# A scan, attention and experts block for four images: the head ordered by hand, mask and residual of the attention as identity matmuls, the group norm at another place in the order

## The chip, the cores and the metric

The kernel runs on one core of a Trainium2 chip. The metric is the device time of one execution in microseconds (us), the median of several executions. PE is the engine of matmuls (PEld its weight loads), DVE the vector engine, ACT the one of activations, POOL GpSimd, SP the one whose queue issues most DMAs. "Tile" here is a named buffer of the program; PSUM is the memory that matmuls write.

## The reference

Four images `x[b]` of 384 channels and 32 x 32 positions (L = 1024 tokens), all in float32. Cut to what matters:

```python
x = x + _L0_conv_ref(_gn(x), ...)          # group norm (32 groups), selective scan, LayerNorm, gelu
t = _to_tokens(x)
t = t + _L1_attn_ref(_ln_t(t), Wq, Wk, Wv)
t = t + _L1_ffn_ref(_ln_t(t), gate_w, gate_b, w1, b1, w2, b2)
```

The selective scan runs over the tokens in four directions k, for 384 channels and 16 states each: `h = h * exp(dt * A) + dt * u * B`, `y = sum over states of h * C`, where dt (softplus of a projection), B and C are projected from the normalised image. The attention has one head of 384, is causal (`where(causal, q k^T * scale, -inf)`, softmax, times v) and is added to t. The last part sends every token through four experts (384 to 1536 to 384, gelu), weighted by a gate of which the two largest of four count.

## The kernel before, in words

A channel group of 32 channels times 4 states fills the 128 partitions. One such group, over all 1024 tokens, is a *unit*; the list `units` has 4 images x 3 blocks of 128 channels (m) x 4 directions (k) x 4 state groups (q) x 4 channel groups (j) = 768. Per unit ACT makes the decay `da` (L442, two units ahead), DVE the product `v` of du = dt*u and B (L449, into PSUM) and the scan `h` (L455), POOL multiplies h by C (L462), and every fourth unit PE sums over states with the matrix `sel` (L487, 16 instructions). The rows of dt and du (128 channels x 1024) and of B and C (`rows`) go out to DRAM and come back spread over the partitions, by DMAs on SP's queue: `dt4` five units ahead, `du4` three, `bc` three (`fetch`, L424 on).

The order of all engines from the first fetches on is written by hand under `tc.manual_schedule()` (L1072): one *tick* t per unit emits the decay of t+2, what was deferred to this tick (`due`), `v` of t, the product of t-1, what stands in `inner`, the scan of t, the sum, the fetches, one step of the preparation of an image, and then other work by generators. A generator yields `("wait", n)` to come back n ticks later or `("pe", n)` to say how many us of PE it has emitted; `go_on` lets the first generator in `waiting` go until the tick's budget is used (`PACE_A` = 4.4 us a tick in attention, `PACE_E` = 3.3 in the experts). Each engine takes its own instructions in the order of emission, and so does SP's queue. PSUM banks (`banks`, 4 of them) and SBUF buffers (`slots`, 8 of them) are taken and given back with the tick; a generator that finds none free waits a tick.

Around the scan:

- **Head** (L140 to L235, `preparation(0)` until its "start", and `fold`). It stands outside the manual schedule, so here the framework orders the instructions. x of image 0 comes on SP's queue, all weights on ACT's. `preparation(b)` (L379): load the image, `groupnorm` (L284: BN_STATS and their sum on DVE, two trips through PE over the groups with `gsel` and `gback`, square root on ACT, normalise on ACT, L312), `project_x` for two pairs of directions (L318: matmuls `pxd`, L328; the two halves of the result copied by ACT to `xd` and `bc`; `bc` stored as `rows`), then `project_dt` (L339) for three blocks and two pairs: matmul, softplus, store, du on DVE (L369), store. In the head this runs up to the first `project_dt`; both pairs' `project_x` come before it. `fold` (L589) then computes g = Wq Wk^T (6 PE groups with ACT copies) and stores it; the first fetches follow.
- **Preparation of image b > 0**: from tick 192 (b-1) + 24 on, one step a tick, group norm included (image b-1 is then being scanned, and image b-2 is in attention).
- **`finish(b)`** (L617): after an image's last unit a LayerNorm (`layernorm`, L517: mean by matmul `mu`, subtract on DVE, L538, squares on ACT, L546, whole width 1024 at once, variance by matmul, L554, reciprocal, spread by matmul `rb`, multiply on DVE, L583), gelu, and the addition of x on DVE (L632).
- **`attention(b)`** (L639), beside the scan of image b+1: LayerNorm, qt and vt (L662, L673), and for eight blocks of 128 queries: `scores` (PE, L691), `softmax` (DVE: add the mask `causal` to the last 128 columns, L702; row maximum, L705; times -scale, L706; ACT: Exp with scale and bias, L710), `normalise` (ACT, L722), `turn` (transposes on PE, copies on ACT, L653), `values` (PE, `po`, L757), and `add` (DVE: three additions of `po` to `yb`, L767, in `inner` of the next tick) with a store.
- **`experts(b)`** (L873): 4 experts x 2 halves of the tokens, `ph` (L947), gelu, `fy` (L972), then DVE (L981, L984).

Work for the last image has no scan beside it: it is a tail.

Of the kernel before, what the change touches and what calls it, by code (L numbers as in the profile page):

```python
# [8 lines left out]
F32 = mybir.dt.float32  # L9
# [38 lines left out]
def hybrid_kernel(  # L48
# [112 lines left out]

    first_x = load_image(0)

    grp = ap0.tile([P, M, C], F32, tag="a0", name="grp")
    nc.scalar.dma_start(grp, group.rearrange("(c p) d -> p c d", p=P))
# [4 lines left out]
    for pair, ks in enumerate(PAIRS):  # L170
        for i, k in enumerate(ks):
            d0, r0 = 64 * pair + 32 * i, 64 - 64 * pair + 32 * i
            for o, w0 in ((d0, 0), (r0, BC0)):
                nc.scalar.dma_start(
                    wx[:, :, pair, o : o + 32],
                    w_x[:, k, w0 : w0 + 32].rearrange("(c p) j -> p c j", p=P),
                )
            nc.scalar.dma_start(wdt[d0 : d0 + R, :], w_dt[:, k, :])
    dtb = const.tile([P, K, M], F32, tag="dtb", name="dtb")
    nc.scalar.dma_start(dtb, dt_bias)  # L180
    lnw = const.tile([P, M], F32, tag="lnw", name="lnw")
    nc.scalar.dma_start(lnw, ln_w)
    lnb = const.tile([P, M], F32, tag="lnb", name="lnb")
    nc.scalar.dma_start(lnb, ln_b)
    dsk = const.tile([P, M, K], F32, tag="dsk", name="dsk")
    nc.scalar.dma_start(dsk, d_skip)
    dsum = const.tile([P, M], F32, tag="dsum", name="dsum")
    nc.vector.tensor_reduce(dsum, dsk, AX.X, ALU.add)
# [3 lines left out]
    nc.vector.tensor_copy(gsel, grp[:, :, :: C // NGRP])  # L192
    gback = const.tile([NGRP, C], F32, tag="gback", name="gback")
    pgb = bank("pgb")
    for m in range(M):
        nc.tensor.transpose(pgb[:NGRP, m * P : (m + 1) * P], gsel[:, m, :], ident)
    nc.scalar.activation(gback, pgb[:NGRP, :C], AF.Copy, scale=float(C // NGRP))


    a_raw = one.tile([P, K * NG, N], F32, tag="yb", name="a_raw")  # L200
    for i in range(NI):
        nc.scalar.dma_start(a_raw[i::NI], a_logs.rearrange("(g d) n -> d g n", d=DJ))
    nc.scalar.activation(a_raw, a_raw, AF.Exp)
    state_i = const.tile([P, NI], F32, tag="state_i", name="state_i")
    nc.vector.tensor_reduce(state_i, ident.rearrange("p (d i) -> p i d", i=NI), AX.X, ALU.add)
    nc.vector.tensor_scalar_mul(state_i, state_i, -1.0)
    a4 = const.tile([P, K * NG, NQ], F32, tag="a4", name="a4")
    nc.vector.memset(a4, 0.0)
    for i in range(NI):
        nc.vector.scalar_tensor_tensor(  # L210
            a4, a_raw.rearrange("p g (q i) -> p g q i", i=NI)[:, :, :, i],
# [947 lines left out]
```

## Time and profile before

The median of 9 runs is 3923.31 us (3918.7 to 3930.33).

| | |
|---|---|
| profiled execution | 3925.99 us |
| its span, first to last instruction | 3924.2 us |
| busy: PE, DVE, ACT, POOL | 3387.2, 3111.6, 1870.3, 1808.1 us |
| mean granted PE clock | 0.890 |
| first L449 of images 0, 1, 2, 3 | 60.4, 800.5, 1633.2, 2463.2 us |
| last L449 | 3250.9 us |
| L455, one scan | 2.285 us |
| L449, one product | 1.233 us |

"Busy" is the sum of an engine's instructions; PE's ends are modelled, so a busy PE isn't PE at its peak. In a table of stretches each engine has its busy us and, in brackets, its instructions. A group of instructions has its line, engine and operation, the tiles out<-in, their shapes and count, then the busy us of all and the mean ns of one, then the idle time of the engine just before them and what ended it. A line of waits has who waited, for whom, us in total, times, and the longest. A line of the timeline has the start, the length and the instruction, with in brackets the idle time before it and what ended it.

### The profile page before, as it was taken

What the parts mean: (1) busy time and instruction counts of PE and PEld (TensorE: products, weight loads), DVE (VectorE), ACT (ScalarE), POOL (GpSimd) and SP (SyncE); (2) the same over time, 40 slices, a digit from 0 to 9 for tenths busy, and PEclk for the clock granted to TensorE, in tenths of its full rate; (3) what the DMA queues carried; (4) which work ended last, traced back from release to release, by engine and by line L of the source; (5) the groups of instructions that cost most, each with busy time, mean ns of one, the idle gap of its engine ahead of it and who ended that gap; (6) DMA issues with size and microseconds to landing.
All of it is one profiled execution on the core that took longest, in us unless ns stands there. A gap on an engine that the chain in (4) does not pass through costs nothing.

```text
span 3924.2 us, 31831 instructions
## 1 busy us (share of the span) xinstructions
PE 3387.2 (86%) x10463; PEld 1369.7 (35%) x10463; DVE 3111.6 (79%) x2348; ACT 1870.3 (48%) x1940; POOL 1808.1 (46%) x776
## 2 busy tenths in 40 slices
PE   5565655558899999988899999788999998999999
PEld 2000100014433334334334334344334344644444
DVE  4999999999899989999999899999999994210000
ACT  5342544444656555545656645545455553332221
POOL 2665666654455556544555556555566651000000
PEclk7555665569999999998899999899999999999999
DMA  5544545453566766544666665535666651132321
GB/s 194 198 146 175 194 155 192 150 183 121 195 213 213 254 206 200 192 158 160 211 223 225 228 226 195 190 105 199 205 207 205 227 189 51 61 90 82 95 82 55
DMA packets 406085, 671.83 MB, mean 171 GB/s; under 512 B 33264, under 2 KB 280352, under 8 KB 405920
## 3 DMA queue, kind: packets, MB, share of 16 engines
q1 hardware_dynamic: 393808, 667.11, 50.0%
q10 hardware_dynamic: 12112, 2.69, 0.4%
q8 instruction: 83, 1.36, 0.1%
q14 instruction: 82, 0.67, 0.0%
HBM read 597.75 MB, written 71.96 MB: 171 GB/s over the span
## 4 chain that ended last, share of the span: by engine, by line
PE 44%; DVE 43%; ACT 5%; issue 5%; DMA 2%; DVEq 0%; POOL 0%; ACTq 0%; SPq 0%; POOLq 0%
DVE h L455 25%; PE ph L947 17%; PE fy L972 15%; DVE v L449 13%; PE y L487 4%; PE pq L662 2%; PE pv L673 2%; PE po L757 1%; ACT da L442 1%; PE ss L691 1%; DMA t2d<-yb 1%; DVE du L369 1%; ACT ht L936 1%; DVE fy L981 1%; ACT L442 1%
## 5 line engine op out<-in xcount | busy, mean ns | idle before, releaser
L462 POOL TENSOR_TENSOR h<-h,bc 128x1024 f32<-128x1024 f32 x768 | 1807.1, 2353 | 1448.5 <-DVE v L449 1345.4
L455 DVE TENSOR_TENSOR_SCAN h<-da,v 128x1024 f32<-128x1024 f32 x768 | 1755.2, 2285 | 84.8 <-DVE v L449 2.4
L442 ACT ACTIVATE da<-dt,a 128x1024 f32<-128x1024 f32 x768 | 877.0, 1147 | 1229.8 <-DVE h L455 1182.5
L972 PE MATMUL fy<-ht,w 128*128 128x512 f32 x2304 | 1027.1, 603 | 1.8 <-ACT dt L361 1.8
L947 PE MATMUL ph<-fx,w 128*128 128x512 f32 x2304 | 1021.4, 599 | 3.6 <-ACT ht L932 3.6
L487 PE MATMUL y<-h,sel 128*32 128x512 f32 x3072 | 710.5, 716 | 331.7 <-POOL h L462 317.9
L449 DVE TENSOR_TENSOR v<-du,bc 128x1024 f32<-128x1024 f32 x768 | 946.7, 1233 | 43.0 <-DMA bc<-rows 14.6
L972 PEld LDWEIGHTS fy<-ht,w 128*128 128x128 f32 x2304 | 439.0, 193 | 582.4 <-issue 563.8
L947 PEld LDWEIGHTS ph<-fx,w 128*128 128x128 f32 x2304 | 433.6, 191 | 577.2 <-issue 527.7
L932 ACT ACTIVATE ht<-ph,b1s 128x512 f32<-128x512 f32 x384 | 257.2, 679 | 496.9 <-PE ph L947 496.5
L487 PEld LDWEIGHTS y<-h,sel 128*32 128x32 f32 x3072 | 117.5, 119 | 875.0 <-POOL h L462 613.9
L981 DVE SCALAR_TENSOR_TENSOR fy<-fy,b2s,tw 128x512 f32<-128x512 f32 x96 | 72.4, 754 | 430.5 <-PE fy L972 430.5
L936 ACT ACTIVATE ht<-ht 128x3072 f32<-128x3072 f32 x64 | 176.8, 2763 | 0.8
L442 ACT ACT_TABLE_LOAD x108 | 138.6, 1283 | 2.0
L691 PE MATMUL ss<-axn,qt 128*128 128x512 f32 (+3 forms) x288 | 108.2, 526 | 15.2 <-ACT pr L710 8.2
L757 PE MATMUL po<-pt,vt 128*128 128x256 f32 x480 | 105.6, 379 | 15.3 <-ACT pt L653 15.3
L757 PEld LDWEIGHTS po<-pt,vt 128*128 128x128 f32 x480 | 90.4, 202 | 31.0 <-ACT pt L653 18.2
L355 PE MATMUL pdt<-xd,wdt 12*128 12x512 f32 x192 | 73.2, 805 | 13.9 <-ACT dt L361 12.2
L691 PEld LDWEIGHTS ss<-axn,qt 128*128 128x128 f32 x288 | 53.3, 204 | 60.7 <-issue 33.8
L984 DVE TENSOR_TENSOR fx<-fx,fy 128x512 f32<-128x512 f32 x96 | 65.9, 686 | 3.3
L936 ACT ACT_TABLE_LOAD x50 | 64.2, 1283 | 0.9
L361 ACT ACTIVATE dt<-pdt,dtb 128x512 f32<-128x512 f32 x96 | 60.6, 683 | 6.2 <-PE pdt L355 5.7
(170 smaller groups left out, 1305.4 us busy)
## 6 DMA issues: line engine op xcount, KB each, us to landing
bc<-rows SPq DMA_DIRECT2D x384, 512.0 KB, 4.8
w<-in_w SPq DMA_DIRECT2D x384, 384.0 KB, 6.0
dt<-dts SPq DMA_DIRECT2D x192, 512.0 KB, 4.2
du<-dts SPq DMA_DIRECT2D x192, 512.0 KB, 6.2
dts<-dt SPq DMA_DIRECT2D x48, 512.0 KB, 3.5
dts<-du SPq DMA_DIRECT2D x48, 512.0 KB, 4.4
fx<-t2d SPq DMA_DIRECT2D x12, 768.0 KB, 6.8
tw<-mkd SPq DMA_DIRECT2D x32, 256.0 KB, 5.9
```

Of the source, the lines that this page charges most:

```text
L442: nc.scalar.activation(u["da"], spread["dt4", n], AF.Exp, scale=a4[:, g, u["q"] : u["q"] + 1])
L449: return nc.vector.tensor_tensor(u["v"], spread["du4", n], spread["bc", n][:, 0, :], ALU.mult)
L455: nc.vector.tensor_tensor_scan(u["h"][:, ::step], u["da"][:, ::step], u["v"][:, ::step], 0.0, op0=ALU.mult, op1=ALU.add,)
L462: product = nc.gpsimd.tensor_tensor(h, h, spread["bc", n][:, 1, :], ALU.mult)
L487: nc.tensor.matmul(y, sel, h, start=first, stop=last, tile_position=(0, jj * DJ))
L691: nc.tensor.matmul(ps[:, : e - o], qt[:, c, i * P : (i + 1) * P], xn[:, c, o:e], start=(c == 0), stop=(c == M - 1),)
L757: nc.tensor.matmul(pv[:, o:], vt[:, j, m * P : (m + 1) * P], pts[step][j // 4][:, j % 4, o:], start=(j == 0), stop=(j == nj - 1),)
L932: nc.scalar.activation(ht[:, f, :], ps, AF.Identity, bias=bias)
L936: nc.scalar.activation(ht, ht, AF.Gelu)
L947: nc.tensor.matmul(ps, tiles[n][:, c, (f % 2) * P : (f % 2 + 1) * P], xns[h][:, c, :], start=(c == 0), stop=(c == M - 1),)
L972: nc.tensor.matmul(pss[m], tiles[n][:, f, :], hts[fh][:, f, :], start=(fh == 0 and f == 0), stop=(fh == 1 and f == FH - 1),)
L981: nc.vector.scalar_tensor_tensor(ps, ps, b2s[:, e, m : m + 1], tw, ALU.add, ALU.mult)
```

## The change

Seven things are changed.

1. **The whole head is under the manual schedule.** x, grp, wx, wdt and dtb come on SP's queue, a_logs alone on ACT's. Exp of a_logs and a dummy Sqrt stand first on ACT. In the group norm of image 0, gsel, its transposes and gback (now a DVE multiply) come after the first block's statistics; block 1 is normalised by DVE. A dummy Softplus and the weights of the scan (`scan_weights`) come before the first projection. Of image 0, DVE makes one of the two copies of pair 0, the read of B and C is issued at once, and `first_dt` makes dt and du for block 0 of pair 0 by halves, storing and fetching direction by direction. Pair 1's projection comes after the start of the ticks.
2. **Weights that are used later, and `fold`, move into the ticks** (`later`, from tick 8 or so), with waits between their steps, on SP's queue. g is scaled by -scale.
3. **The scores come with the sign turned and scaled**: the mask is +1e30, and PE adds it with a matmul of `ident` and `causal` into the last 128 columns. DVE takes a minimum in place of the maximum, and instead of L706 (32 times) a minimum of two columns where a row has two pieces (16 times). Exp has scale -1.
4. **The residual of attention goes in by PE**: a matmul of `ident` and `yb` (256 columns) opens each `po`; ACT copies `po` to `yb` (512 and 256 columns a step), in `due` of the next tick.
5. **Squares of the LayerNorm by halves of 512 columns.**
6. **The preparation of image b steps on as soon as that of b-1 is over**, through load and group norm, and waits only then for tick 192 (b-1) + 24.
7. `fetch` can be told which of its three reads to issue.

The core of the diff:

```diff
+    ctx.enter_context(tc.manual_schedule())
     first_x = load_image(0)
-    nc.scalar.dma_start(grp, group.rearrange("(c p) d -> p c d", p=P))
+    nc.sync.dma_start(grp, group.rearrange("(c p) d -> p c d", p=P))
+    a_raw = one.tile([P, K * NG, N], F32, tag="yb", name="a_raw")
+    for i in range(NI):
+        nc.scalar.dma_start(a_raw[i::NI], a_logs.rearrange("(g d) n -> d g n", d=DJ))
...
+    def group_weights():
+        nc.vector.tensor_copy(gsel, grp[:, :, :: C // NGRP])
+        pgb = bank("pgb")
+        for m in range(M):
+            nc.tensor.transpose(pgb[:NGRP, m * P : (m + 1) * P], gsel[:, m, :], ident)
+        return pgb
...
+    nc.scalar.activation(a_raw, a_raw, AF.Exp)
+    nc.scalar.activation(dump, eps, AF.Sqrt)
...
-        out=causal, in_=causal, compare_op=ALU.is_ge, fill=NEG, base=0,
+        out=causal, in_=causal, compare_op=ALU.is_ge, fill=-NEG, base=0,
...
+    def later():
+        yield "wait", 8
+        for t, src in (
...
+        ):
+            nc.sync.dma_start(t, src)
+            yield "wait", 1
+        yield "wait", 2
+        nc.vector.tensor_reduce(dsum, dsk, AX.X, ALU.add)
+        yield from fold()
@@ groupnorm
+            if b == 0 and m == 0:
+                pgb = group_weights()
             yield "wait", 1
+        if b == 0:
+            nc.vector.tensor_scalar_mul(gback, pgb[:NGRP, :C], float(C // NGRP))
...
+            if b == 0 and m == 1:
+                nc.vector.tensor_scalar(
+                    u[m], u[m], rstd[:, m : m + 1], mean[:, m : m + 1], ALU.mult, ALU.add
+                )
@@ new
+    def first_dt(u, xd):
+        ks = PAIRS[0]
+        dts = [slots.now(f"dt_0_{k}_0", P, L) for k in ks]
+        dus = [slots.now(f"du_0_{k}_0", P, L) for k in ks]
+        pss = {(i, h): banks.now(f"pdt_0_{i}_{h}") for h in range(NH) for i in range(2)}
+        for (i, h), ps in pss.items():
+            r = slice(32 * i, 32 * i + R)
+            nc.tensor.matmul(ps, wdt[r, :P], xd[r, bass.ts(h, 512)], start=True, stop=True)
+        for i, k in enumerate(ks):
+            for h in range(NH):
+                s = bass.ts(h, 512)
+                nc.scalar.activation(
+                    dts[i][:, s], pss[i, h], AF.Softplus, bias=dtb[:, k, 0:1]
+                )
+                nc.vector.tensor_mul(dus[i][:, s], dts[i][:, s], u[0][:, s])
+            nc.sync.dma_start(dts_d[0, k][0, :P, :], dts[i])
+            nc.sync.dma_start(dts_d[0, k][1, :P, :], dus[i])
+            if i == 0:
+                for t in (-5, -4):
+                    fetch(t, ("dt4",))
+                    fetch(t + 2, ("du4",))
+        for t in (-3, -2, -1):
+            fetch(t, ("dt4",))
+            if t < -2:
+                fetch(t + 2, ("du4",))
...
@@ preparation
         yield from groupnorm(b, u)
+        while clock[0] < IMAGE * (b - 1) + 24:
+            yield "wait", 1
         xd = one.tile([P, L], F32, tag="xd", name=f"xd_{b}")
-        for pair in range(2):
-            yield from project_x(b, pair, u, xd)
+        if b == 0:
+            nc.scalar.activation(dump, eps, AF.Softplus)
+            scan_weights()
+        yield from project_x(b, 0, u, xd)
+        if b == 0:
+            fetch(-3, ("bc",))
+            first_dt(u, xd)
+            yield "start", 0
+        yield from project_x(b, 1, u, xd)
@@ layernorm
-            nc.scalar.activation(sq, dst[:, c, :], AF.Square)
             sqs.append(sq)
+        for h in range(n):
+            for c in range(M):
+                s = bass.ts(h, 512)
+                nc.scalar.activation(sqs[c][:, s], dst[:, c, s], AF.Square)
@@ attention
+                if e > i * P:
+                    nc.tensor.matmul(ps[:, e - o - P : e - o], ident, causal, start=False, stop=True)
...
-            last = ss[-1][2]
-            nc.vector.tensor_add(last[:, -P:], last[:, -P:], causal)
...
-                nc.vector.tensor_reduce(nb[:, n : n + 1], ps, AX.X, ALU.max)
-            nc.vector.tensor_scalar(
-                nb[:, 0:1], nb[:, 0:1], nb[:, len(ss) - 1 : len(ss)], -scale, ALU.max, ALU.mult
-            )
+                nc.vector.tensor_reduce(nb[:, n : n + 1], ps, AX.X, ALU.min)
+            if len(ss) == 2:
+                nc.vector.tensor_tensor(nb[:, 0:1], nb[:, 0:1], nb[:, 1:2], ALU.min)
...
+                nc.tensor.matmul(pv, ident, yb[:, m, s], start=True, stop=False)
...
-                for m in range(M):
-                    nc.vector.tensor_add(yb[:, m, s], yb[:, m, s], pos[m])
+                for m in range(0, M, 2):
+                    n = min(2, M - m)
+                    nc.scalar.copy(
+                        yb[:, m : m + n, s],
+                        pos[m // 2][:, : n * TQ].rearrange("p (m t) -> p m t", m=n),
+                    )
...
-            defer(1, add, inner)
+            defer(1, add)
@@ ticks
-            if preps and t >= IMAGE * (B - 1 - len(preps)) + 24:
+        if preps:
```

## The prediction

> **What bounds the kernel now.** First the chain that ended last, then busy time by stretch, cut where the timeline of DVE shows an image's first L449 multiply (60.4, 800.5, 1633.2, 2463.2 us), 72 ticks after the second of these, where image 0's attention is over, and in the tail.
>
> ```profile
> PE 44%; DVE 43%; ACT 5%; issue 5%; DMA 2%; DVEq 0%; POOL 0%; ACTq 0%; SPq 0%; POOLq 0%
> ```
>
> ```profile
> 0.00:60.40 60.40, 33.62 (x103) 17.93 (x103) 11.66 (x33) 26.90 (x35) 1.09 (x8) 0.92 0.63 192
> 60.40:800.50 740.10, 431.99 (x886) 67.55 (x884) 706.70 (x426) 325.55 (x299) 447.71 (x191) 0.60 0.50 178
> 800.50:1145.80 345.30, 276.56 (x1090) 130.66 (x1091) 313.98 (x291) 179.77 (x212) 169.41 (x73) 0.86 0.47 164
> 1145.80:1633.20 487.40, 481.38 (x1445) 192.12 (x1444) 456.71 (x287) 287.40 (x275) 282.82 (x121) 0.99 0.65 221
> 3254.80:3454.50 199.70, 183.21 (x742) 104.36 (x741) 56.76 (x116) 63.44 (x102) 2.38 (x2) 0.95 0.19 61
> 3454.50:3924.20 469.70, 463.76 (x1082) 205.01 (x1080) 36.21 (x59) 99.82 (x102) 0.00 (x0) 1.00 0.27 79
> ```
>
> Columns: stretch, length, then PE, PEld, DVE, ACT, POOL busy, PE clock, DMA share, GB/s. No engine is full in the head. Image 0's scan is DVE-bound: 706.7 of 740.1 us, 95.5%, is DVE full with its gaps. Beside attention DVE falls to 91% and PE to 80% at clock 0.86: they wait for each other. Beside the experts PE is 98.8% and DVE 93.7% busy, both near full. The last experts are PE alone. So the end is set by head + 740 + three intervals of some 830, 830, 788 us + a PE tail of 673.
>
> What ends the head, and what DVE waits for beside image 0's attention:
>
> ```profile
> 59.56 0.33 SPq L613 DMA_DIRECT2D g_d<-g_s  x1
> 60.38 1.23 DVE L449 TENSOR_TENSOR v<-du,bc 128x1024 f32<-128x1024 f32 x1 [14.58 <-DMA bc<-rows]
> 66.37 1.23 DVE L449 TENSOR_TENSOR v<-du,bc 128x1024 f32<-128x1024 f32 x1 [2.36 <-DMA du<-dts]
> ```
>
> ```profile
> DVE ss L702 <- PE ss L691: 6.3, 2, 5.2
> DVE yb L767 <- PE po L757: 5.1, 2, 2.6
> DVE du L369 <- PE ph L947: 3.6, 1, 3.6
> ```
>
> The first multiply waits 14.6 us for rows that stand behind four stores and four reads in SP's queue. The second is late because SP sat at fold's store (L613) until 59.6 before it issued more du reads. The operations that leave DVE:
>
> ```profile
> L767 DVE TENSOR_TENSOR yb<-yb,po 128x256 f32<-128x256 f32 x48 | 17.7, 414 | 26.4 <-PE po L757 26.4
> L702 DVE TENSOR_TENSOR ss<-ss,causal 128x128 f32<-128x128 f32 x32 | 9.4, 293 | 61.9 <-PE ss L691 61.9
> L706 DVE TENSOR_SCALAR nb<-nb 128x1 f32<-128x1 f32 x32 | 6.9, 214 | 1.1
> ```
>
> **What the Trainium skill says.** "TensorE: Matmul & The Clock Gate" (What's actually happening): PE runs at half clock until some 3.4 us of activity. The head agrees: L328's loads came every 0.85 us from 27.1 to 29.7, then every 0.43. "ScalarE: Activation LUTs" (What ACT_TABLE_LOAD costs): 1283 ns a load, and the trace has 1283. "DMA: Bandwidth & Descriptors" (Queues, rings and completion order): SP and ACT each own one ring on the same 16 engines, which take turns between them, so a_logs on ACT's queue still takes time from x on SP's; the trace before never has these two together.
>
> **Head, worked out.** a_logs costs about 4 us of all engines: the DMA share is 80 to 90% from 15.8 to 20.3 us, where little else moves. It now runs beside x (landed by 9.3 us before), and grp comes after x on SP. I take gsel at 11.5 us instead of 5.9. Between zero and full overlap this is 8.5 to 12.5. Then DVE copies gsel (0.24) and has four BN_STATS (0.67) and two aggregates (0.21), 3.1 us; gback by DVE (0.5, as on ACT) and a copy (0.17) bring it to 15.5. The group chain without its waits, from the rows at 11.5 to 20.1: 0.7 to the mean's copy and 1.6 for the way back, 0.8 for four small DVE steps, and 2.3 for the variance: 5.4 us, so 20.9. Sqrt's table is already loaded; 0.3+0.5 us more and the scale stands at 21.7 against 23.9. What is saved (the wait for gback until 15.6, for a_raw's Exp and a table until 22.6) is half spent on the later grp.
>
> From there: three normalise steps of 1.17 on ACT become two, with one on DVE. That tensor_scalar isn't in the trace; "VectorE: DVE Perf Modes" (The perf-mode tier table) lets fp32 tensor_scalar run 2x, so an estimate from 0.61 (half of L449's time) to 1.23 (all of it); 1.0 taken, hidden beside ACT's first. First L328 at 23.0 (25.2 before), half clock for six matmuls, 5.1 us, then 2.6: pair 0 ends at 30.7 (33.0). Only then the order changes: pair 1's projection (6 us of ACT and PE) no longer precedes dt. dt's matmuls of the first half run during the second xd copy; the third of four ends at 33.3 (0.86 each), Softplus (0.65, table loaded by 25.4) at 34.0, the half multiply (0.65) at 34.7: du of k=0 is done there, against 44.7. SP: rows store at 31.5, landing 2.9 later; bc issues for 1.25 to 35.7; two stores to 36.4, landing 3.2 to 4 later (bc's 1 MB goes ahead at about 400 GB/s, as the head's DMA slices reach 390 to 419), 40.4; dt4 and du4 reads issue by 42.2 (1.15 and 0.64) and land some 2.4 us later. First L449 at **44.6**, against 60.4: −15.8. After it 3 MB of stores and reads feed units 1 to 3 at one per 2.6 to 4 us against a 3.7 us tick, so the 2.3 us stall before unit 1 stays about as it was. The fold (18 transposes, 18 matmuls, 9 ACT moves of 0.48, two 576 KB loads, one store) and seven small loads move into the ticks past SP's dt, du and bc reads: ACT is 44% and DMA 50% busy there and da runs two ticks ahead; zero taken. If that cover went, 4.4 us of ACT. **Head −15.8** (−8 to −20).
>
> **Group norm moved.** Per image DVE has 6 x 0.67 + 3 x 0.21 + small steps = 6.0 us. For image 1 nothing moves in kind (tick 24 either way). For image 2 it goes from beside image 0's attention into image 0's scan, where DVE is full: +6.0 there. For image 3 from beside image 1's attention to beside its experts, where DVE has 2% of slack: +4 there. SP is asked for x earlier (three loads of 512 KB, waiting for u's last reader, with dt and bc reads behind): 0, at worst 3 us each.
>
> **Attention beside a scan.** Per image off DVE: 12 x 0.414 + 8 x 0.293 + 8 x 0.214 less 4 x 0.144 = 8.4 us. With L767 goes its wait: 5.1 us for images 0 and 1, 0.4 for image 2. The wait of L702 for PE passes to the reduce behind it (L705) and stays. ACT takes the copies: per image 4 x (0.57 + 0.36) = 3.7 us. ACT's copy now waits for po, and queued behind it are Exp (L710) and pt's copies; da is two ticks ahead, so DVE isn't reached. PE gets 8 identity matmuls of 128 columns and 12 of 256, two instructions each; from 72 of 512 columns in 30.9 us, 0.429 each: 8 x 0.215 + 12 x 0.43 = 6.9 us an image. PE idles 69 us in image 0's stretch (part of it on ACT's pt, 5.5 us, which the identity matmul comes ahead of). Squares by halves: six of 0.62 for three of 1.05, +0.6 us ACT, but the last half ends 1.3 us sooner after DVE's subtract; not counted beside the scan. With the group norm, DVE loses 8.4+5.1+6.0 = 19.5, 19.5 and 8.8 us. What becomes late next is PE (80% busy, +7) and ACT's copy chain, so I keep three quarters: **−14.6, −14.6+4, −6.6**; bounds all (−19.5) and a quarter.
>
> **Tail.** PE gets the same 6.9 us in a PE-bound stretch. Against it: var_at waits 3.7 us for squares, of which 2 goes; po's 2.3 us wait on pt is partly filled by the identity; DVE's two steps of 0.5 ahead of Exp go. **+3** (−1 to +7). Attention's longer budget (12 x 0.43 at 4.4 a tick, 1.2 ticks) pushes some 4 us of image 2's experts past the last scan, into the 5.7 us for which PE waits on L632; zero.
>
> **Sum.** −15.8 + 6.0 − 14.6 − 10.6 − 6.6 + 3 = **−38.6**. The profiled execution took 3925.99 us (span 3924.2 and 1.8 around it), so 3887.4; it stands 2.7 over the median of 3923.31, so **3885** for a median.
>
> **Rivals.** (1) *Attention is paced by the PE-ACT chain, not DVE*: for, PE's waits on ACT (var_at 9.8, pt 5.5) and 80% PE; against, DVE's 91%. Then what DVE loses returns as its waits for PE: head −15.8, group norm +6 +4 −12, half of 4 x 6.9 = +13.8: −4, 3919. 17%. (2) *DVE's waits shrink too*: the waits at L702 (6.3 per image) and du go with a PE that starts values without waiting; −19.5, −15.5, −8.8, three times −4, +6, head −17, tail 0: −66.8, 3857. 17%. (3) *Slower*: image 2's and 3's projections now begin at tick +24, not some 17 later, in the middle of attention; each takes 3 to 4 of 8 slots and 1 or 2 of 4 banks, and attention yields a tick whenever it finds none. Each tick lost beyond the 3 in hand (image 1's experts end at 2501.6, 38 us or 10 ticks into image 3; the next attention waits for L632 until 2522) pushes 3.3 us of experts into the PE tail. It decides from about 12 net ticks (38.6 / 3.3); at 15, 3934. For: they share the pools. Against: preparation held the same pools later in attention. 6%.
>
> **How the numbers follow.** Forecast 60%. The range is 3856 to 3916: it leaves out half of (2), half of (1) and (3). A measurement tells 0.2% (7.8 us) from no change: below 3915.5 lie the forecast, (2) and a third of (1), 0.83; within 0.2% the rest of (1), 0.11; slower, (3), 0.06.
>
> **What would show it.** First L449 near 44.6; image 1's first L449 near 791 (−15.8 + 6); stretches of 72 ticks of about 330 us in place of 345 and 343; no wait at a yb add on DVE; PE from the last scan to the end some 3 us longer. It is wrong if DVE's busy share beside attention falls (then (1)), or if experts reach past tick 13 of an image's scan (then (3)).

## The result, and the profile after

The kernel after the change takes 3910.12 us (median of 9 runs, 3907.11 to 3914.71) against 3922.51 us before (29 runs): a ratio of 0.9969, 95% interval 0.996 to 0.9977. That is 12.4 us gained where 38.6 was forecast: the direction is right and the time lies inside the stated range (3856 to 3916), but two thirds of the gain did not come. The profiled execution has a span of 3909.6 us, 14.6 less than before. All the accounting below is made on spans; where a median says something else, it says so.

The chain that ended last has shifted from PE to DVE:

```profile
DVE 49%; PE 38%; issue 5%; ACT 4%; DMA 2%; DVEq 1%; POOL 1%; SPq 0%; POOLq 0%; ACTq 0%
```

Busy time by stretch, cut at the same events as before (the first product `v`, now L512, of images 0 and 1, 72 ticks later, and so on; columns as in the prediction):

```profile
0.00:49.72 49.72, 20.72 (x59) 10.21 (x59) 14.31 (x37) 13.85 (x17) 1.09 (x8) 0.91 0.64 168
49.72:790.10 740.38, 424.10 (x928) 73.00 (x928) 706.79 (x427) 335.45 (x314) 447.79 (x191) 0.61 0.50 180
790.10:1126.00 335.90, 279.20 (x1125) 136.26 (x1126) 310.25 (x268) 183.66 (x226) 169.64 (x73) 0.88 0.49 174
1126.00:1613.50 487.50, 480.65 (x1454) 192.34 (x1453) 461.30 (x305) 290.73 (x277) 282.81 (x120) 0.98 0.67 226
1613.50:1958.00 344.50, 299.88 (x1210) 147.53 (x1209) 312.27 (x259) 197.22 (x239) 169.75 (x73) 0.94 0.50 172
3237.30:3439.00 201.70, 190.34 (x768) 109.18 (x767) 47.89 (x78) 70.29 (x117) 2.40 (x2) 0.95 0.19 61
3439.00:3909.60 470.60, 464.69 (x1102) 206.90 (x1100) 38.15 (x72) 99.79 (x103) 0.00 (x0) 1.00 0.27 79
```

The head is 10.7 us shorter (60.4 to 49.7) and the attention of image 0 is 9.4 shorter (345.3 to 335.9). The attention of image 1 (1613.5 to 1958.0) is 1.8 us *longer* than before (342.7): PE has more work there (299.9 us, 293.8 before) and DVE less (312.3 us, 317.3 before), yet the stretch didn't shrink. Beside the forecast, part by part:

| part of the span, us | forecast | after | three repairs (below) |
|---|---|---|---|
| head, to the first product | -15.8 | -10.7 | -15.9 |
| scan of image 0 | +6.0 | +0.3 | -1.0 |
| interval of image 1 (image 0's attention and experts) | -14.6 | -9.3 | -14.5 |
| interval of image 2 | -10.6 | +3.0 | +0.1 |
| interval of image 3 | -6.6 | -0.8 | -5.1 |
| tail after the last product | +3 | +2.9 | +3.5 |
| sum | -38.6 | -14.6 | -32.9 |

The last column is the best kernel of the experiments, 3892.03 us: three small edits bring most of what the change seemed to have lost. It lands near the forecast in four rows, but that doesn't make the forecast's steps right: one of the edits changes the order in the head, which the forecast had otherwise.

What DVE waits for in image 0's attention, and then in image 1's (waiting instruction, releaser, us, times, longest):

```profile
DVE nb L780 <- PE ss L771: 6.7, 3, 4.7
DVE nb L780 <- PE ss L766: 2.8, 1, 2.8
```

```profile
DVE nb L780 <- PE ss L771: 11.5, 4, 10.3
DVE axn L601 <- DMA out<-fx: 9.5, 1, 9.5
```

No wait at a yb add is left, as forecast. But the row minimum (L780) waits longer than the mask's add did (6.3 and 6.4 us before): in image 1's attention its longest wait is 10.3 us, where the mask's add waited 5.2. And a wait stands there that was nowhere beside a scan before: the LayerNorm of the attention (L601) waits 9.5 us until the *previous* image's output is stored, since the two share a buffer. The experts of image 0 added their last result at tick 13 of the scan of image 2 before, and now at tick 16.

The long wait for the scores has its reason on PE. DVE stops at 1744.46 us, and what PE does until the scores are there is this (three of its groups), with the end of DVE's wait in this kernel and in the kernel before:

```profile
1744.49 2.74 PE L350 MATMUL pxd<-x,wx 128*128 128x512 f32 x6
1750.95 2.84 PE L350 MATMUL pxd<-x,wx 128*128 128x512 f32 x6
1753.63 0.83 PE L766 MATMUL ss<-axn,qt 128*128 128x128 f32 x6
1754.72 0.29 DVE L780 TENSOR_REDUCE nb<-ss 128x1 f32<-128x128 f32 x1 [10.26 <-PE ss L771]
```

```profile
1759.09 0.30 DVE L702 TENSOR_TENSOR ss<-ss,causal 128x128 f32<-128x128 f32 x1 [5.18 <-PE ss L691]
```

`pxd` is the projection of image 3. With its group norm done early it starts two ticks after the wait for tick +24 ends, at tick +26 of image 2's scan, and stands on PE right ahead of the scores; before, it came at ticks +41 to +47, after them. The 5.58 us of `pxd` cover the 5.1 us by which the wait grew. The experiments below confirm it: with the group norm at its old place this wait is 5.0 to 5.4 us (four kernels), with the early group norm 10.1 to 10.8 (twelve kernels).

Cut into DVE's work and DVE's idle time, the three 72-tick stretches of attention beside a scan give (length = busy + idle, from the traces of the five kernels; "head alone" and "group norm late", the kernel after with the group norm at its old place, are experiments below):

| 72 ticks beside a scan | before | head alone | after | group norm late | three repairs |
|---|---|---|---|---|---|
| attention of image 0 | 345.3 = 314.0 + 31.3 | 340.8 = 314.2 + 26.6 | 335.9 = 310.2 + 25.7 | 340.3 = 311.5 + 28.8 | 334.1 = 307.7 + 26.4 |
| attention of image 1 | 342.7 = 317.3 + 25.4 | 341.6 = 317.4 + 24.2 | 344.4 = 312.2 + 32.2 | 341.6 = 315.1 + 26.5 | 341.2 = 309.4 + 31.8 |
| attention of image 2 | 326.7 = 309.1 + 17.6 | 328.0 = 309.3 + 18.7 | 325.9 = 307.7 + 18.2 | 326.5 = 307.5 + 19.0 | 321.3 = 303.0 + 18.4 |

Three things are read from it. DVE lost only 3.8, 5.1 and 1.4 us of work, not 8.4. The wait at the yb add is gone from the list, but it is no gain in idle time: image 0's idle time is 26.6 us already with the head alone, where the add is still on DVE and still waits 5.1 us. And the 6.8 us of idle time that came in image 1's attention come with the group norm's new place: 25.4, 24.2 and 26.5 with the old one, 32.2 and 31.8 with the new.

**Where DVE's missing saving is.** One row of the new groups is far dearer than it should be, the minimum of two columns that stands in place of the scaling:

```profile
L782 DVE TENSOR_TENSOR nb<-nb 128x1 f32<-128x1 f32 x16 | 13.9, 866 | 0.5
```

I had priced it at 0.144 us. Its sixteen instructions take from 0.158 to 1.712 us each; the four in the tail, where POOL has nothing to do, all take 0.16. The timeline of DVE and then of POOL shows what a long one stands beside:

```profile
2589.33 0.14 DVE L795 RECIPROCAL nb<-nb 128x1 f32<-128x1 f32 x1
2589.45 1.23 DVE L512 TENSOR_TENSOR v<-du,bc 128x1024 f32<-128x1024 f32 x1
2590.59 0.88 DVE L780 TENSOR_REDUCE nb<-ss 128x1 f32<-128x512 f32 x2
2591.51 1.71 DVE L782 TENSOR_TENSOR nb<-nb 128x1 f32<-128x1 f32 x1
2593.15 2.27 DVE L518 TENSOR_TENSOR_SCAN h<-da,v 128x1024 f32<-128x1024 f32 x1
```

```profile
2590.86 2.35 POOL L525 TENSOR_TENSOR h<-h,bc 128x1024 f32<-128x1024 f32 x1 [1.63 <-DVE v L512]
```

The minimum starts at 2591.51, inside POOL's product, and ends at 2593.22; the product ends at 2593.21. "SBUF — State Buffer" (Who interferes with whom) of the Trainium skill says that a DVE instruction with two inputs in SBUF (the memory of all tiles that aren't in PSUM) contends with a POOL instruction that reads SBUF, and that the port pair they share is an exclusive lock. This trace agrees: of the twelve beside a scan, eleven start while a POOL product runs, ten of these take 0.67 to 1.71 us and end within 0.02 us of that product's end, and the eleventh starts in the product's last 0.11 us and takes 0.16. The reduce just before, with its input in PSUM, isn't held up.

### The profile page after: what moved, and what is told of

It is laid out like the page before. It is cut to its first block, busy times and chain, and to the rows that moved or that the text cites. A ratio compares the mean times of both kernels' runs of the same rounds, so it can differ in the third digit from the quotient of the medians.

```text
span 3909.6 us, 32087 instructions
## 1 busy us (share of the span) xinstructions
PE 3385.5 (87%) x10623; PEld 1393.1 (36%) x10623; DVE 3099.6 (79%) x2258; ACT 1887.6 (48%) x1996; POOL 1808.5 (46%) x776
## 4 chain that ended last, share of the span: by engine, by line
DVE 49%; PE 38%; issue 5%; ACT 4%; DMA 2%; DVEq 1%; POOL 1%; SPq 0%; POOLq 0%; ACTq 0%
DVE h L518 29%; DVE v L512 16%; PE ph L1027 14%; PE fy L1052 13%; PE y L550 3%; PE ss L766 2%; PE pq L737 2%; PE pv L748 2%; PE po L832 1%; DVE fy L1061 1%; ACT da L505 1%; PE pxd L350 1%; ACT ht L1016 1%; DVE du L395 1%; DMA du<-dts 1%
## 5 line engine op out<-in xcount | busy, mean ns | idle before, releaser
L1052 PE MATMUL fy<-ht,w 128*128 128x512 f32 x2304 | 1014.6, 597 | 2.7 <-ACT dt L387 0.9
L512 DVE TENSOR_TENSOR v<-du,bc 128x1024 f32<-128x1024 f32 x768 | 947.0, 1233 | 39.4 <-DMA du<-dts 17.4
L550 PE MATMUL y<-h,sel 128*32 128x512 f32 x3072 | 693.2, 714 | 307.0 <-POOL h L525 292.1
L381 PE MATMUL pdt<-xd,wdt 12*128 12x512 f32 x184 | 71.0, 805 | 35.1 <-ACT xd L354 27.7
L780 DVE TENSOR_REDUCE nb<-ss 128x1 f32<-128x512 f32 (+3 forms) x48 | 26.1, 553 | 78.5 <-PE ss L771 62.5
```

The costliest lines, as they stand in the source:

```text
L512: return nc.vector.tensor_tensor(u["v"], spread["du4", n], spread["bc", n][:, 0, :], ALU.mult)
L550: nc.tensor.matmul(y, sel, h, start=first, stop=last, tile_position=(0, jj * DJ))
L1052: nc.tensor.matmul(pss[m], tiles[n][:, f, :], hts[fh][:, f, :], start=(fh == 0 and f == 0), stop=(fh == 1 and f == FH - 1),)
```

## The experiments

Each kernel is compared with the one before the change; ratios carry a 95% interval, 3 to 5 us either way. The kernel before had medians from 3922.6 to 3926.1 us beside them, so a difference of less than some 5 us between two experiments is not firm by the medians alone. Stretches and waits are read from one trace of each kernel. Unless said otherwise the base is the kernel after.

**The minimum by another instruction.** The same result with one tensor input and a column as scalar:

```diff
-                nc.vector.tensor_tensor(nb[:, 0:1], nb[:, 0:1], nb[:, 1:2], ALU.min)
+                nc.vector.tensor_scalar(
+                    nb[:, 0:1], nb[:, 0:1], nb[:, 1:2], 1.0, ALU.min, ALU.mult
+                )
```

> One change to the kernel after: the minimum of two columns (L782) is a tensor_scalar with the second column as its per-partition scalar, as L706 was before, in place of a tensor_tensor. In the kernel after, twelve of these sixteen stand beside a scan and take up to 1.7 us, each to the moment at which POOL's product ends. Theory A (a DVE operation that reads two SBUF tensors stands until POOL is done, and DVE sets the pace beside attention): 0.2 us each, about 13 us of DVE gone, time 3897 to 3902. Theory B (PE sets the pace there, the long minimum is hidden): also 0.2 us each, but time 3907 to 3911 and longer waits of the row minimum (L780) for PE. Theory C (the length belongs to the tile or the shape, not to POOL): the tensor_scalar is as long.

Measured: 3905.01 us, 0.9948 (0.9936 to 0.996), 5.1 us less than the kernel after (span 7.1 less), between Theories A and B; C is refuted. Every one of the 16 now takes 0.21 us, beside POOL or not:

```profile
L782 DVE TENSOR_SCALAR nb<-nb 128x1 f32<-128x1 f32 x16 | 3.4, 214 | 0.6
```

**The minimum on all rows.** The opposite: the same tensor_tensor on every row block, 32 times, where it is needed 16 times.

```diff
-            if len(ss) == 2:
-                nc.vector.tensor_tensor(nb[:, 0:1], nb[:, 0:1], nb[:, 1:2], ALU.min)
+            k = len(ss) - 1
+            nc.vector.tensor_tensor(nb[:, 0:1], nb[:, 0:1], nb[:, k : k + 1], ALU.min)
```

> The kernel after with the suspected cost doubled: the tensor_tensor minimum also for the 16 rows of blocks with one piece (the minimum of a column with itself, same result). Theory A (it stands until POOL's product ends, and DVE sets the pace): twelve more beside a scan, of 0.7 to 1.7 us each, +8 to +15: 3918 to 3925. If half of it is taken up by waits for PE, as the run with the tensor_scalar suggests: +4 to +7, 3914 to 3917. Theory C (POOL has no part in it): 0.16 us each, time as after.

Measured: 3931.65 us, 1.0019 (1.0011 to 1.0027): 21.5 us more than the kernel after, more than Theory A's +8 to +15, and slower than before the change. The group grew by 16.0 us, since the added ones take up to 2.18 us; the rest wasn't traced to a cause:

```profile
L782 DVE TENSOR_TENSOR nb<-nb 128x1 f32<-128x1 f32 x32 | 29.9, 934 | 1.1
```

Sixteen instructions on one column each cost more than the whole change had gained.

**The old budget of the values.** The change counts one more matmul group per block (`0.43 * (nj + 1)`), so attention takes more ticks and the experts end later.

```diff
-                yield "pe", 0.43 * (nj + 1)
+                yield "pe", 0.43 * nj
```

> One change to the kernel after: the identity matmuls of the residual are left out of attention's declared PE time (0.43 nj a block again). Theory A (attention takes 1.2 ticks longer by its budget, so the experts of image 1 end 2 to 3 ticks later and the first write to axn in the shared buffer waits 9.5 and 2.2 us for the store of out): these two waits go or shrink below 3 us together, time 3900 to 3905. Theory B (experts end late because of banks and slots, not of the budget): waits stay, time 3908 to 3912.

Measured: 3910.85 us, 0.9962 (0.995 to 0.9975), no change. The last expert sums moved from ticks 16 and 15 to 15 and 14 and the 9.5 us wait fell to 2.9, but others came in its place. DVE's waits in this kernel between 1613.5 and 1958 us:

```profile
DVE nb L780 <- PE ss L771: 12.0, 4, 10.8
DVE du L395 <- ACT dt L387: 5.2, 1, 5.2
DVE axn L601 <- DMA out<-fx: 2.9, 1, 2.9
```

The stretch itself was 347.2 us, 344.4 in the kernel after. So the 9.5 us wait, which looked like the cause of image 1's bad stretch, isn't one that can be had for itself: when it shrank, the time was waited elsewhere, and the 10.8 us wait for the scores stayed.

**The new head alone.** The kernel before with only the head (and the weights moved into the ticks) of the kernel after; old group norm, mask, residual and squares.

```diff
-        while clock[0] < IMAGE * (b - 1) + 24:
-            yield "wait", 1
...
+            nc.vector.tensor_add(last[:, -P:], last[:, -P:], causal)
...
-                nc.tensor.matmul(pv, ident, yb[:, m, s], start=True, stop=False)
...
+                    nc.vector.tensor_add(yb[:, m, s], yb[:, m, s], pos[m])
...
+            nc.scalar.activation(sq, dst[:, c, :], AF.Square)
```

> The kernel before with the new head alone: mask, sign, residual, squares and the place of the group norm as before. If the parts add up: first product at 49.7 us and time 3912 to 3914 (10.7 us less than before), the tail 673 us again, so all of the other parts together give about 2 us in the kernel after. If the other parts had gained much and the head cost something later, this would be near 3920.

Measured: 3910.11 us, 0.996 (0.9947 to 0.9972), the same as the whole change. The four other parts together gave nothing that the medians show: by spans -5.4 in the interval of image 1, +4.6 in that of image 2, -2.8 in that of image 3 against this kernel. Its tail is 675.8 us, not the expected 673: 2.5 longer than before, though it has no identity matmul.

**The rows read after the first stores.** In the head the read of B and C (`bc`, 1 MB) was issued ahead of the stores of dt and du, and these landed behind it.

```diff
-            fetch(-3, ("bc",))
             first_dt(u, xd)
...
             if i == 0:
+                fetch(-3, ("bc",))
                 for t in (-5, -4):
```

> One change to the kernel after: the read of B and C (1 MB) for the first unit is issued after the first direction's stores of dt and du, not before them. Theory A (the head's loss against the forecast is the landing of these stores behind that read, 42.7 in place of 40.4, and of the du read behind it): stores issued at 32.5 to 33.2, landed by 37.5, first product at 43 to 45 in place of 49.7, time 3903 to 3906. Theory B (bytes decide: 3 MB must move before the first product whatever the order): first product at 48 to 50, time as after.

Measured: 3907.75 us, 0.9953 (0.9939 to 0.9966); the first product is 6.2 us earlier (Theory A) and the span 5.5 shorter, the median 2.4. The kernel after had an unlucky head: over all kernels of this case the new order's first product comes at 43.3 us on average and the old order's at 47.7, so the order is worth some 4.4. SP's queue in the kernel after, and DVE at the end of its head:

```profile
34.22 1.23 SPq L484 DMA_DIRECT2D bc<-rows  x2
35.53 0.54 SPq L421 DMA_DIRECT2D dts<-dt  x1
36.17 0.38 SPq L422 DMA_DIRECT2D dts<-du  x1
42.90 0.52 SPq L473 DMA_DIRECT2D dt<-dts  x1
44.13 0.52 SPq L473 DMA_DIRECT2D du<-dts  x1
```

```profile
49.72 1.23 DVE L512 TENSOR_TENSOR v<-du,bc 128x1024 f32<-128x1024 f32 x1 [15.26 <-DMA du<-dts]
```

and the same two in this kernel:

```profile
32.56 0.33 SPq L421 DMA_DIRECT2D dts<-dt  x1
33.28 0.32 SPq L422 DMA_DIRECT2D dts<-du  x1
34.36 1.49 SPq L484 DMA_DIRECT2D bc<-rows  x2
35.94 0.57 SPq L473 DMA_DIRECT2D dt<-dts  x1
37.36 0.51 SPq L473 DMA_DIRECT2D du<-dts  x1
```

```profile
43.54 1.23 DVE L512 TENSOR_TENSOR v<-du,bc 128x1024 f32<-128x1024 f32 x1 [9.08 <-DMA du<-dts]
```

The read of du is issued 6.8 us earlier (37.36, 44.13), because the store of dt that the reads wait for is in flight for at most 3 us (32.89 to 35.94) in place of 7 (36.07 to 42.90). The read itself still takes some 6 us in both (44.13 to 49.72, 37.36 to 43.54).

**The three edits together** (minimum, budget, rows):

> The kernel after with three edits together: minimum by tensor_scalar, old budget, read of B and C after the first stores. Alone they took the span by 7.1, 1.0 and 5.5 us under that of after (head luck of 1 to 2 us in each). If they add: 3896 to 3899. If what DVE wins beside attention only becomes a wait for PE, the first and third alone count: 3899 to 3903.

Measured: 3892.03 us, 0.9922 (0.9911 to 0.9934), better than both kernels and than the sum of the parts: 30 us less than before and 18.1 less than after. Its attention of image 0 and of image 1:

```profile
783.67:1117.76 334.09, 277.98 (x1131) 135.57 (x1132) 307.66 (x268) 183.71 (x226) 169.57 (x73) 0.89 0.50 176
1601.90:1943.10 341.20, 302.32 (x1203) 148.58 (x1202) 309.38 (x257) 195.64 (x237) 169.68 (x73) 0.93 0.51 173
```

Against the kernel after, DVE is busy 2.6, 2.9 and 4.7 us less in the three stretches of attention while its idle time is about the same (table above): the minimum. Alone the edits had brought 5.1, nothing and 2.4 us, so I took each out of the three:

> The kernel after with the minimum as a tensor_scalar and the broadcast rows read after the first stores, and with the new, longer budget for the values left as it is; it lacks only the budget of the best kernel so far (3892.0). If the budget is what lets the repairs count (experts spill less, no wait for the output's store), this is 4 us or more slower: 3896 to 3902. If the budget is worth nothing, as it was alone (3910.9 against 3910.1), the time is 3892 within its interval, and the minimum and the rows make the 18 us together.

> The best kernel so far with the two-column minimum put back as the tensor_tensor of the kernel after: only that one instruction, 16 times, differs from 3892.0, and against the kernel with the mask on DVE (3909.2) only the mask and the sign. If the minimum's standing is worth what the DVE trace lists, about 3 us in each of three images and what follows from it, this takes 3900 to 3906. If the gain of 18 us came from elsewhere, it stays below 3896.

Measured without the old budget: 3898.59 us, 0.9943 (0.993 to 0.9957); without the new minimum: 3903.05 us, 0.9951 (0.9938 to 0.9963). Both lie in their first expectation. So beside the others the minimum is worth 11.0 us and the old budget 6.6, of which 5.1 of span lie in the interval of image 1 (823.3 to 818.2), not where the 9.5 us wait stood. That the budget brings nothing alone and 6.6 beside the two is more than the medians' scatter suggests, but the intervals don't exclude that part of it is scatter.

**The residual back on DVE** (the three additions of `po` to `yb`, without identity matmul and ACT copy), and, from the best kernel, **no residual at all**:

```diff
-                nc.tensor.matmul(pv, ident, yb[:, m, s], start=True, stop=False)
...
+                    nc.vector.tensor_add(yb[:, m, s], yb[:, m, s], pos[m])
```

> The kernel after with the residual of attention on DVE again (three additions a step in the inner order, no identity matmul, old budget); mask, sign, squares, group norm and head as after. Theory A (DVE sets the pace beside attention): the three attention stretches longer by 4 us of additions and up to 5 of waits each, the tail 3 to 5 us shorter, so 3917 to 3925. Theory B (the wait for po passes to the row minimum and PE gets as much work as DVE loses): stretches within 2 us of after, tail 3 to 5 us shorter, 3903 to 3909.

> The best kernel so far without the attention residual: the identity matmuls of the values are left out and nothing takes their place, so the output lacks the residual after attention; ACT still copies the result and DVE has nothing to do. It asks what PE's 12 identity matmuls of 256 columns per image (estimated at 5.2 us) cost beside a scan. If PE and what follows it pace attention, each of the four images gives back 4 to 5 us: about 3873. If DVE paces it and PE has room, only the tail gives it back: about 3887.

Measured: on DVE 3914.15 us, 0.9979 (0.9969 to 0.9989), between the two theories: 4.0 more than after, and 3.3 more than the kernel with the old budget (3910.85), from which it differs in the residual alone. With no residual 3889.9 us, 0.9916 (0.9902 to 0.9929), 2.1 less than the best kernel. In the second, the tail gives 2.5 us back and the three intervals -3.1, -0.7 and +2.1: no cost of PE's 12 identity matmuls per image is seen beside a scan. In the first, against the kernel with the old budget, DVE is busy 4.8, 3.7 and 3.2 us more in the three stretches of attention and idle 0.7 to 1.0 us *less*. The yb adds wait for PE again there (3.0, 6.0 and 0.4 us), and other waits shrink by as much. So the move saves DVE's work and no idle time, and some 3 to 4 us in all, since the tail pays 3.6 us for it.

**The mask and the sign on DVE again**, with the old budget and the rows after the stores, so that it differs from the best kernel in the mask and sign alone:

```diff
+            last = ss[-1][2]
+            nc.vector.tensor_add(last[:, -P:], last[:, -P:], causal)
...
-                nc.vector.tensor_reduce(nb[:, n : n + 1], ps, AX.X, ALU.min)
+                nc.vector.tensor_reduce(nb[:, n : n + 1], ps, AX.X, ALU.max)
```

> The kernel after with the mask and the sign as before (the causal mask added by DVE, maximum, combination by tensor_scalar on all eight rows, no identity matmul for the mask), and with the old budget and the rows read after the first stores; it differs from the best kernel so far only in the mask and the sign. If DVE paces attention, three images lose the 8 adds of 0.29 and 4 combinations, some 2.5 to 3 us each, while the tail gains PE's 1.7: about 3898 to 3900. If the mask on PE gives nothing, because its wait for PE passes to the row minimum, the time stays within 3 us of 3892.

Measured: 3909.18 us, 0.9965 (0.9951 to 0.9979), 17.2 more than the best kernel, where 6 to 8 was the larger expectation. In the three stretches DVE is busy 2.7, 2.6 and 3.1 us more, as counted, and idle 4.8, 3.3 and 3.1 us more (31.2, 35.1 and 21.5). So the move of the mask takes waiting away too, though which wait isn't shown: the long wait for the scores in image 1's attention is 10.6 us here as well. With the minimum as the change has it (3903.05), 11.0 of these 17.2 us are lost again.

**The group norm at its old place**, from the kernel after and from the best one:

```diff
-        while clock[0] < IMAGE * (b - 1) + 24:
-            yield "wait", 1
...
-        if preps:
+        if preps and t >= IMAGE * (B - 1 - len(preps)) + 24:
```

> The kernel after with the preparation of image b held back to tick 192 (b-1) + 24 as a whole, as before; all else as after. Theory A (the group norm beside attention costs DVE 6 us, once it is gone from interval 2): image 1's scan interval unchanged or 3 us shorter (it loses the group norm of image 3), image 2's 3 to 6 us longer, time 3911 to 3917. Theory B (the earlier projections take banks and slots from attention, which then ends later): the last accumulations of an image's experts at tick 14 of the next image in place of 16, the wait for the store of out under 4 us in place of 9.5, time 3903 to 3909.

> The best kernel so far (minimum as a tensor_scalar, old budget for the values, broadcast rows read after the first direction's stores) with image 2's and 3's group norms back at the old time. If the early group norms cost image 2's attention beside image 1's scan (in that kernel the interval of image 2 is still 830.1 us, with one wait of 2.2 us for the output's store; with the late group norm alone it was 825.9), this gains 2 to 5 us more: 3887 to 3890. If moving group norm costs nothing, the time stays at 3892 within its interval.

Measured: 3908.02 us, 0.9964 (0.9952 to 0.9976), and 3893.96 us, 0.9927 (0.9915 to 0.994): 2.1 less and 1.9 more, no difference in all. Inside, it moves time between intervals, the same way in both: image 2's is 7.1 and 8.2 us shorter, image 1's 5.7 and 5.4 longer (image 3's 0.5 and 3.7 longer, the tail 0.0 and 1.8). Theory B's signs came in both: the last expert sums are back at tick 13, no attention waits at L601 for the output's store beside a scan for more than 0.4 us, and the projection of image 3 is at ticks +42 to +48, with the wait for the scores ahead of it at 5.4 and 5.0 us. The idle time of image 1's attention is 26.5 us in both, and 31.2 to 37.8 us in all twelve kernels with the early group norm, whatever else was changed in them. That the total stays is not explained; experts that spill three ticks further lengthen the next interval and shorten their own, which fits, but no run separates it.

**The squares whole again**, from the best kernel:

```diff
-        for h in range(n):
-            for c in range(M):
-                s = bass.ts(h, 512)
-                nc.scalar.activation(sqs[c][:, s], dst[:, c, s], AF.Square)
+            nc.scalar.activation(sq, dst[:, c, :], AF.Square)
```

> The best kernel so far with the squares of each layer norm taken whole again, three of 1.05 us in place of six of 0.62. If the halves let PE start the variance sooner where it matters (1.3 us for each wide norm, four images, the tail above all), this is 2 to 6 us slower: 3894 to 3898. If ACT's extra 0.6 us cancels it, no change: 3892 within its interval.

Measured: 3893.71 us, 0.9927 (0.9915 to 0.994), 1.7 more: not to be told from nothing. In the tail it is visible: PE's wait for the squares there is 4.0 us with whole squares and 1.0 with halves, and the tail 3.1 us longer.

## Why the prediction was right or wrong

The direction and the head's chain on the engines held. What failed, with what the runs showed: the price of the new minimum (0.144 us forecast, 1.1 beside a scan), the wait that was to go with L767 (5.1 us for images 0 and 1; no idle time went), the place of image 3's group norm (its projection came ahead of the scores, 7 to 8 us in the interval of image 2), and in the head the du read (2.4 us forecast, 5.6 came) behind stores that landed late.

**The head (-15.8, came -10.7).** The chain on the engines held: the group norm's scale stood at 20.4 us (forecast 21.7), the rows were stored at 31.3 (31.5), and du of the first direction was ready by 33.3 (34.7). DVE's normalising step, which no trace had, took 0.81 us, inside the estimate of 0.61 to 1.23. What failed is the step "landing 3.2 to 4 later (bc's 1 MB goes ahead ...), 40.4; dt4 and du4 reads issue by 42.2 ... and land some 2.4 us later". The read of dt could issue only at 42.9 and that of du at 44.1, 1.9 us late, and the du read took 5.6 us in place of 2.4. 1.9 + 3.2 is the 5.1 us of this trace. The rows experiment shows the first half by removing it (reads 6.8 us sooner). The second was mis-sized from the start: the page of the kernel before has all such reads at a median of 6.2 us from issue to landing.

```profile
du<-dts SPq DMA_DIRECT2D x192, 512.0 KB, 6.2
```

How much was lost is in part luck: over all kernels with the rows after the stores the first product came at 41.5 to 44.5 us (eight profiles), over the others with this head at 46.0 to 49.7 (seven), of which the kernel after is the latest. That the best kernel's head meets the forecast is luck too: its order is another, and its du read takes some 7 us (issued at 37.18, product at 44.52).

**The group norm moved (+6.0 in image 0's scan; off image 0's and image 1's attention 6.0 each; +4 beside experts).** "For image 2 it goes from beside image 0's attention into image 0's scan" is wrong: its BN_STATS went from ticks 219 to 221 only to 207 to 209, which is still in the attention, because the preparation before it ends shortly before. The trace of before had that: image 1's last du stands at tick 187. Image 0's scan is 0.3 us longer, not 6. For image 3 it went from tick 411 to 340, beside image 0's experts and not image 1's. Its 6 us did leave image 1's attention, but what they were to be worth there did not come, because of a step that the sum put at nothing: the projections no longer wait for the group norm. They come some 16 ticks sooner, ahead of the scores that DVE waits for, and six products du (7.5 us) fall into the 72 ticks where four (5.0 us) did. Measured by taking the move back, it costs 7.1 and 8.2 us in the interval of image 2, where -4.5 (three quarters of 6.0) and +4 were forecast. It gives 5.7 and 5.4 in that of image 1, where -4.5 was forecast for a group norm that in fact stayed there. The forecast's terms for this move add up to +1.0 and the measured total is about 0: the agreement is chance.

**Attention beside a scan (-14.6, -14.6, -6.6; came -9.3, +3.0 (forecast with group norm -10.6), -0.8).** Beside the group norm's part, three terms failed.
- *"less 4 x 0.144"*, the price of the new minimum. I took it from small DVE rows that stand where POOL is idle. Beside a scan it took 1.1 us on average (0.158 to 1.712), 4.4 us an image instead of 0.6. This is shown: another instruction of the same meaning gains 5.1 us, and 11.0 beside the other repairs; doubling it costs 21.5.
- *The 8.4 us* of DVE's work: with the minimum mended and the group norm at its old place, DVE's busy time is 6.5, 6.2 and 6.2 us less than with the head alone. I had summed the durations of instructions, and neighbours overlap in the trace: L795 above ends at 2589.47, L512 begins at 2589.45 and ends at 2590.68, L780 begins at 2590.59. The row of L767 in the prediction shows it too: 48 of 414 ns are 19.9 us, its busy time is 17.7.
- *"With L767 goes its wait: 5.1 us for images 0 and 1"*: the wait goes from the list and no idle time goes with it. With the residual on DVE again and all else equal, idle time is 0.7 to 1.0 us less, not 5 more: other waits give way. From head alone to the best kernel with the group norm at its old place, which takes all of these moves together, idle time changed by +0.2, +2.3 and +3.3 us.

So of the 13.6 us that the interval of image 2 lacks, 7.1 to 8.2 came with the group norm's move, against 0.5 of gain forecast for it. For the rest, the minimum's price (1.7 us in this interval when mended alone, 4.5 beside the other repairs) and three quarters of the 5.1 us wait are of the right size; this sum is an estimate.

*"The wait of L702 for PE passes to the reduce behind it (L705) and stays"* erred the other way. The wait is still there, but the mask's move, measured alone, took 3 to 5 us of idle time an image with it. *"Pushes some 4 us of image 2's experts past the last scan ...; zero"*: the budget was not free, though not at that place; it cost 6.6 us once the minimum was mended, most of it in image 0's attention and experts.

**The tail (+3)** came as +2.9, but this is no evidence for its terms: with the head alone, without one identity matmul, the tail is 2.5 us longer too. Taken alone, the residual's matmuls cost 3.6 us there, and the squares by halves save 3.1.

**The rivals.** Rival 1, that the PE-ACT chain paces attention, gave 3919; the time lies between it and the forecast. The cost of the residual's matmuls on PE is not seen beside a scan: leaving them out frees 2.1 us by the median, about what the tail alone gives back (2.5). What ACT's copies cost was not tried alone. The rival's sign, DVE's busy share falling, is there in image 1's attention only (92.6% to 90.6%; 90.9% to 92.4% in image 0's), but part of what DVE saved did come back as idle time, as above. Rival 2, that waits shrink too, holds for the mask. Rival 3 had the right event, projections that begin at tick +24 "in the middle of attention", and experts that spill past tick 13, to 16; the cost came through PE's time ahead of the scores, and in the total it is balanced by image 1's interval.

With the three repairs, head, image 1's interval, image 3's and the tail are each within 1.5 us of the forecast; as said, for the head, the tail and image 1's interval this is partly chance. The two prices that failed most could have been read from the traces of before: the du read's from its own row, and the minimum's by asking what POOL does beside it.

## What to carry to other kernels

When a small operation is put in place of another, ask not only how long it is but whose memory port it needs while which other engine runs: a one-column instruction with two SBUF inputs lasted until POOL's product ended, and cost 11.0 of the 17.2 us that the move of the mask gains. Price a new instruction from a row that stands beside the same neighbours, and count savings from an engine's busy time, not from the sum of its durations. A long wait in the list isn't yet a cause: take it away, and see whether another comes in its place. And when a step is moved earlier, follow what was waiting behind it: here the projection behind the group norm landed on PE ahead of the scores.

## What the hardware showed that was not expected

- A tensor_tensor minimum of two 128x1 columns in SBUF takes 0.16 us with POOL idle and up to 2.18 us (in the kernel with 32 of them) while POOL multiplies 128x1024 elements; the tensor_scalar form, its second column given as a scalar, took 0.21 us in all 16 cases.
- A DVE reduce from PSUM beside the same POOL product wasn't lengthened: 0.55 us on average for L780 before and after the minimum was changed.
- One read of 512 KB that spreads over the partitions took 5.6 and 6.2 us when it was one of four issued within 3 us of each other; the median of the 192 such reads of du in the kernel before is 6.2.
